# Bias network of a deformable attention: one third-layer matmul for four keys, met by DMA

## The chip, the cores and the metric

The kernel runs on one core of a Trainium2 chip. The metric is the device time of one execution in microseconds (us); lower is better. TensorE (PE), VectorE (DVE), ScalarE (ACT), GpSimd (POOL) and SyncE (SP) each work through their own list of instructions in order. SP and POOL here mostly issue DMAs.

## The reference

Four network layers follow one another on x of shape (2, 512, 32, 32): a deformable attention with an MLP, a linear attention, a non-local block and a squeeze-and-excite block. Only the first one's position bias matters here. For each of 8 groups (4 head pairs x 2 images; the kernel calls one g) there are 64 keys, 512 in all, and 1024 queries, and two heads' queries per key are handled together. For every pair of query and key a small network maps the relative position to a bias:

```python
pos = grid_q[:, :, None, :] - grid_kv[:, None, :, :]
bias = jnp.sign(pos) * jnp.log1p(jnp.abs(pos))
bias = jax.nn.relu(bias @ cpb_w1 + cpb_b1)     # 2 -> 128
bias = jax.nn.relu(bias @ cpb_w2 + cpb_b2)     # 128 -> 128
bias = (bias @ cpb_w3 + cpb_b3)                # 128 -> 1
sim = jnp.einsum('bhid,bhjd->bhij', qh, kh) + bias
attn = jax.nn.softmax(sim, axis=-1)
```

So the third layer is a sum of 128 hidden outputs with weights, for 512 keys x 2048 columns. All is float32.

## The kernel before, in words

**The bias stage.** The loop goes over 256 pairs of keys, `p`. For each key `n`, `first` (L351, VectorE) makes the first layer's 128 x 2048 tile `h1`; `tabp` tables for eight keys at a time are loaded by SP and scaled by ScalarE (L172). For a pair, `second(p, o)` runs four times, for four quarters `o` of the 128 hidden units: two keys x four matmuls into a `ph` tile (L617; 32 output columns of TensorE each, four side by side), then the relu by ScalarE (L626) into a tile `r{o}` of 128 x 2 x 512. The rows of such a tile are 4 column blocks x 32 hidden units, its middle index is the key of the pair. There are 4 buffers for `r0`, 3 for `r2`, one each for `r1` and `r3`.

**Sums before the third layer.** The weights of the third layer have been folded into the second layer and hidden units have been permuted so that units with equal sign of weight stand together. So outputs can simply be added before the last matmul: `combine` (L632, VectorE) adds `r1` to `r0` and `r3` to `r2` with a sign `rel`; `join` (L635) adds `r2` to `r0` by an accumulating DMA on POOL; `shift` (L642, two DMAs on SP) copies half of the rows of each key into a tile `xs` of 128 x 512, and `fold` (L647, two accumulating DMAs on POOL) adds the other half. After that one `xs` tile holds a pair's two keys, interleaved by rows, 16 rows per column block and key. `third(g, u)` (L656) multiplies four `xs` tiles by `cw3`, a narrow matrix of signs, one matmul per pair, four of them into the four 32-row blocks of a `psim` tile.

**The order of work.** Everything in the stage is pinned to program order. The loop runs `second(p, o)` for o = 0 to 3; `first` for the keys of the next pair comes at o = 0 and 2, `combine(p-1, 2)` and `join(p-1)` at o = 1, `combine(p, 0)` at o = 3. All else is put into this loop by a table written by hand: `at(n, when, fn, ...)` places a step at key n (when 0 is after the even o, when 1 after the odd one). Steps placed so are `shift(p)` at key 2p+4, `fold(p)` at 2p+5, `third`, the table loads, the sampling of keys and values for the next group (`prepare`), the softmax of the last group (`attend`: transposes, maxima, exponentials, sums) and the offset network of later groups (`chain`, whose 36 taps at L229 are spread over 80 and 116 keys). `psb` (L584) spreads signs and biases over the 128 rows once at the start; `spread_out` (L480) copies them and makes `cw3`.

After the stage the attention's output projection (L1035), the MLP (L1100) and the other layers follow; they don't touch the change.

Of the kernel before, what the change touches and what calls it, by code (L numbers as in the profile page):

```python
# [27 lines left out]
MID = C // 4  # L28
SE = C // 16
EPS = 1e-5  # L30
FMAX = float(np.finfo(np.float32).max)


# [21 lines left out]

_CONSTS = [("ident", P), ("grid", 2 * J), ("gridf", J), ("npx", 1), ("npy", 8), ("sel3", 2)]

_ORDER = [("same", P), ("below", P), ("place", P), ("rank", 1), ("third", 35)]
_CAT, _n = {}, 0
for _name, _w in _CONSTS:  # L60
    _CAT[_name] = (_n, _w)
# [10 lines left out]
def conv_seq(  # L72
# [61 lines left out]
    with ExitStack() as ctx_l0:  # L134
# [3 lines left out]
        kblk = l0.tile([P, 2, 2, J], F32, name="kblk")  # L138
        vblk = l0.tile([P, 2, 2, J], F32, name="vblk")

        co = l0.tile([P, 2, 2, KC * B * J], F32, name="co")
# [44 lines left out]
        def pin(ins):  # L186
            return tc.keep_in_program_order(ins) if started else ins
# [12 lines left out]
        class Chain:  # L200


            def __init__(self, k0, k1, alloc):
                self.k0, self.n, self.alloc = k0, (k1 - k0) * P, alloc
                self.g = slice(k0 * B, k1 * B)
                self.cs = slice(k0 * P, k1 * P)
                self.sums = {}

            def tile(self, name):
# [123 lines left out]

        w2a = l0.tile([P, 4, 32], F32, name="w2a")
        sb3 = l0.tile([P, 4, 2], F32, name="sb3")
        cw3 = l0.tile([P, 35], F32, name="cw3")
        rel = l0.tile([P, 2], F32, name="rel")

        h1p = ctx_att.enter_context(tc.tile_pool(name="h1p", bufs=4))
# [21 lines left out]
        with tc.tile_pool(name="a", bufs=1) as a, tc.tile_pool(name="aps", bufs=3, space=PSUM) as aps, tc.tile_pool(  # L363
# [80 lines left out]
            def oc(name):  # L444
                at, w = _CAT[name]
                return ordc[:, at : at + w]
# [6 lines left out]
            wide = a.tile([P, 4, 4, 32], F32, name="wide")  # L453
# [6 lines left out]
            def counted():  # L460
                pin(ve.tensor_copy(od[:, 7:9], pcnt))
                pin(ve.tensor_scalar(cpbw, cpbw, maj, None, ALU.mult))


                pin(ve.tensor_scalar(maj, total, 4.0, None, ALU.is_ge))
                pin(ve.tensor_scalar(t0, maj, -1.0, 1.0, ALU.mult, ALU.add))
                pin(ve.tensor_scalar(t1, total, -1.0, 8.0, ALU.mult, ALU.add))
# [109 lines left out]
            for k in range(2, KC):  # L577
                for t in range(NT // 512):
                    flip_x(k, t, (dve, act)[t % 2])
                    if (k, t) == (2, 1):  # L580
                        psb = apk.tile([P, 4, 2], F32, name="psb", tag="pfb4")
# [13 lines left out]
        with tc.tile_pool(name="hid", bufs=3) as hid, tc.tile_pool(name="sm", bufs=1) as sm, tc.tile_pool(name="hps", bufs=2, space=PSUM) as hps, tc.tile_pool(  # L595
# [6 lines left out]
            def at(n, when, fn, *args):  # L602

                todo.setdefault((n, when), []).append((fn, args))
# [44 lines left out]
            def third(g, u):  # L649
                kb, i = divmod(u, 4)  # L650
                p = (g * J + 8 * u) // 2
                if i == 0:
                    psims[g, kb] = sps.tile([P, 512], F32, name=f"psim{kb}")
                for m in range(4):
                    pin(
                        nc.tensor.matmul(  # L656
                            psims[g, kb][m * 32 : (m + 1) * 32, :],
                            lhsT=cw3[:, 3 - i : 35 - i],
                            rhs=rs.pop(p + m),
                            start=(i == 0),  # L660
                            stop=(i == 3),
                            skip_group_check=True,
                        )
                    )

            def prepare(g):

                k, b = divmod(g, B)
                st = {}
                n = J * (g - 1) + 30  # L670
                def hat(t):
                    if t == 0:
                        st["smp"] = smpp.tile([P, 8, 2, J], F32, name="smp")
                    pin(
                        nc.scalar.activation(
                            st["smp"][:, t],
                            co[:, 1, :, g * J : (g + 1) * J],
                            AF.Abs,
                            bias=c("npy")[:, t : t + 1],
                        )  # L680
                    )
# [4 lines left out]

                def cross(i):
                    sp = st["smp"][:, 4 * i : 4 * i + 4]
                    hx = co[:, 0, :, g * J : (g + 1) * J]
# [30 lines left out]
                def keys():  # L720

                    for h in range(2):
                        hs = slice(h * DH, (h + 1) * DH)
                        pin(
                            nc.scalar.activation(
                                kblk[hs, g % 2, h, :].rearrange("p (k x i) -> p k x i", k=2, i=4),
                                st["pk"][hs, 0, :].rearrange("p (k i x) -> p k x i", k=2, i=4),
                                AF.Identity,
                                scale=DH**-0.5,
                            )  # L730
                        )

                def values():
                    for h in range(2):
                        hs = slice(h * DH, (h + 1) * DH)
                        pin(
                            nc.vector.tensor_copy(
                                vblk[hs, g % 2, h, :].rearrange("p (k x i) -> p k x i", k=2, i=4),
                                st["pk"][hs, 1, :].rearrange("p (k i x) -> p k x i", k=2, i=4),
                            )  # L740
                        )

# [154 lines left out]
                    )  # L897
            for g in range(NG):
                prepare(g)
                for u in range(8):  # L900
                    at(J * g + 8 * u + 14, 0, third, g, u)
                if g < NG - 1:
                    attend(g, J * (g + 1) + 7, True)
            for p in range(NK // 2):
                at(2 * p + 4, 0, shift, p)
                at(2 * p + 5, 0, fold, p)

            def chain(k0, k1, n, taken):
                ch = Chain(k0, k1, lambda shape, name: mps.tile(shape, F32, name=name, tag="m"))
# [970 lines left out]
def _layout(a):  # L1880
# [50 lines left out]
    rank = p // 32 * 2 + p % 2  # L1931
    same = p[:, None] % 32 // 2 == p[None] % 32 // 2
    put("same", same.astype(f), order)
    put("below", (same & (rank[:, None] < rank[None])).astype(f), order)
    put("place", np.array([0, 1, 4, 5, 2, 3, 6, 7])[rank].astype(f)[None], order)
    put("rank", rank.astype(f)[:, None], order)
    put("third", (np.arange(35)[None] == (3 + 8 * (p // 32) + 4 * (p % 2))[:, None]).astype(f), order)
    put("npy", -(4 * np.arange(8)[None] + p[:, None] // 32).astype(f))


# [54 lines left out]
```

## Time and profile before

| | us |
|---|---|
| three runs | 2724.93, 2726.71, 2727.19 |
| median | 2726.71 |
| profiled execution, own time | 2726.49 |
| its span, first to last instruction | 2724.7 |
| second-layer matmuls L617, busy | 1781.7 |
| first layer L351, busy | 1171.1 |
| relu L626, busy | 1141.6 |
| combine L632, busy | 656.2 |
| third-layer matmuls L656, busy (512 records) | 70.5 |
| join L635, 256 issues, issue to landing (median) | 4.8 |
| shift L642, 512 issues, issue to landing (median) | 2.2 |
| fold L647, 512 issues, issue to landing (median) | 4.7 |
| TensorE / VectorE / ScalarE / POOL busy, share of span | 98% / 83% / 56% / 25% |

A matmul in float32 leaves two records, so 512 records at L656 are 256 matmuls. Busy time of a group counts the time in which at least one of its instructions ran; records of one engine may overlap, so a sum of records can be more than the time that the engine needs. In lines of groups, the columns are: line, engine, operation, output<-input, shape and count, then busy us, mean ns of one, and idle time before them with what ended it. In timelines a line begins with the start in us and the length in us. The bias stage runs from 44 to about 1942 us at a full TensorE clock.

### The profile page before, as it was taken

How to read it: one execution, taken by the hardware profiler on the slowest of the kernel's cores; microseconds unless marked ns; L12 is line 12 of the kernel's file. 1: busy time of each engine (PE TensorE's matmuls, PEld its weight loads, DVE VectorE, ACT ScalarE, POOL GpSimd, SP SyncE). 2: the span in 40 equal slices, each digit the busy share in tenths (PEclk: the TensorE clock that was granted, in tenths of full speed). 3: DMA queues.
4: the chain of work that ended last, by engine and by line, in shares of the span. 5: the costliest groups of instructions: out<-in, count | busy, mean ns of one | idle time of the engine just before them, and what ended most of it. 6: DMA issues, size and time to landing. Idle time of an engine off the chain costs nothing.

```text
span 2724.7 us, 49360 instructions
## 1 busy us (share of the span) xinstructions
PE 2681.3 (98%) x19830; PEld 978.1 (36%) x19830; DVE 2253.8 (83%) x1993; ACT 1538.4 (56%) x1904; POOL 670.2 (25%) x784
## 2 busy tenths in 40 slices
PE   8999999999999999999999999999999999999997
PEld 4223323232332323333333233333344444455544
DVE  6999999999999999999999999999554544615646
ACT  7676687667668766866766776776221111001334
POOL 0333333333333333333333333333100000000001
PEclk9999999999999999999999999999999999999998
DMA  3777777877777787777787788787410000100001
GB/s 128 165 167 164 161 157 156 172 154 161 168 155 160 155 174 155 161 167 157 168 193 164 157 174 189 156 172 157 94 30 23 16 23 24 39 38 1 0 0 62
DMA packets 146196, 335.13 MB, mean 123 GB/s; under 512 B 22672, under 2 KB 32400, under 8 KB 145200
## 3 DMA queue, kind: packets, MB, share of 16 engines
q0 software_dynamic: 77824, 201.38, 41.5%
q1 hardware_dynamic: 67568, 130.08, 13.6%
q8 instruction: 157, 2.57, 0.4%
q14 instruction: 71, 0.58, 0.1%
q10 hardware_dynamic: 576, 0.51, 0.1%
HBM read 58.99 MB, written 4.46 MB: 23 GB/s over the span
## 4 chain that ended last, share of the span: by engine, by line
PE 89%; DVE 6%; issue 3%; ACT 2%; DMA 0%; DVEq 0%; POOL 0%; ACTq 0%; POOLq 0%
PE ph L617 58%; PE A L1100 4%; PE D L1100 4%; PE C L1100 4%; PE B L1100 2%; PE psim L656 2%; PE po L1035 2%; DVE h L351 2%; DVE r L632 2%; PE pg L1243 1%; PE pa L1354 1%; PE pu L1277 1%; PE pscore L1486 1%; PE pz L1515 1%; PE pt L1506 1%
## 5 line engine op out<-in xcount | busy, mean ns | idle before, releaser
L617 PE MATMUL ph<-h,w2a 128*32 128x512 f32 x16384 | 1781.7, 592 | 4.3 <-ACT r L626 3.6
L626 ACT ACTIVATE r<-ph,sb 128x1024 f32<-128x1024 f32 x1024 | 1141.6, 1115 | 533.2 <-PE ph L617 508.1
L351 DVE CUSTOM_DVE_ANT_1 h<-tab 128x2048 f32<-128x2048 f32 x512 | 1171.1, 2287 | 22.4 <-PE ph L617 17.7
L617 PEld LDWEIGHTS ph<-h,w2a 128*32 128x32 f32 x16384 | 522.2, 109 | 1219.8 <-issue 832.0
L632 DVE SCALAR_TENSOR_TENSOR r<-r,rel,r 128x1024 f32<-128x1024 f32 x512 | 656.2, 1282 | 26.8 <-ACT r L626 26.5
L647 POOL DMA_DIRECT2D xs<-r x512 | 475.0, 1128 | 225.7 <-DMA xs<-r 122.7
L635 POOL DMA_DIRECT2D r<-r x256 | 222.6, 869 | 1047.8 <-DVE r L632 874.5
L172 ACT ACTIVATE tab<-tab,vec 128x256 f32<-128x256 f32 x252 | 137.1, 544 | 0.0
L1288 POOL MEMSET M<- 128x512 f32 x2 | 1.0, 518 | 443.8 <-DVE x L1164 443.8
L1140 ACT COPY u<-A 128x512 f32<-128x512 f32 x16 | 9.4, 586 | 146.9 <-PE A L1100 146.9
L1771 POOL TENSOR_TENSOR x<-x,aff 128x512 f32<-128x512 f32 x7 | 7.0, 1029 | 329.1 <-ACT e L1736 329.1
L1119 ACT ACTIVATE h<-h,vec 128x512 f32<-128x512 f32 x32 | 23.1, 721 | 113.6 <-DVE h L1122 113.6
L656 PE MATMUL psim<-xs,cw 128*32 128x512 f32 x512 | 70.5, 594 | 2.2 <-DMA xs<-r 2.2
L1122 DVE TENSOR_TENSOR h<-C,u 128x512 f32<-128x512 f32 x32 | 22.1, 691 | 47.7 <-PE C L1100 47.4
L1100 PE MATMUL A<-xn,w 128*128 128x512 f32 x128 | 60.3, 593 | 0.8 <-DVE x L1042 0.8
L1100 PE MATMUL C<-hT,w 128*128 128x512 f32 x128 | 60.3, 592 | 0.0
L1100 PE MATMUL A<-h,w 128*128 128x512 f32 x128 | 60.1, 592 | 0.0
L1035 PE MATMUL po<-q,vwo 128*128 128x512 f32 x128 | 57.1, 599 | 0.0
L229 DVE SCALAR_TENSOR_TENSOR acc<-q,vec,acc 128x128 f32<-128x128 f32 (+3 forms) x88 | 45.9, 521 | 0.8
L1160 DVE TENSOR_TENSOR x<-D,x 128x512 f32<-128x512 f32 x32 | 22.1, 691 | 26.0 <-PE D L1100 26.0
L852 ACT ACTIVATE e<-e,den 128x64 f32<-128x64 f32 x128 | 41.8, 337 | 2.2 <-DVE den L848 2.2
L1160 DVE TENSOR_TENSOR x<-C,x 128x512 f32<-128x512 f32 x32 | 22.1, 691 | 24.8 <-PE C L1100 24.8
(364 smaller groups left out, 1840.3 us busy)
## 6 DMA issues: line engine op xcount, KB each, us to landing
r<-r POOLq DMA_DIRECT2D x256, 512.0 KB, 4.8
xs<-r SPq DMA_DIRECT2D x512, 128.0 KB, 2.2
xs<-r POOLq DMA_DIRECT2D x512, 128.0 KB, 4.7
tab<-fd SPq DMA_DIRECT2D x63, 512.0 KB, 6.2
lw<-in_l_w_dram SPq DMA_DIRECT2D x5, 1024.0 KB, 9.1
x<-in_x_dram SPq DMA_DIRECT2D x4, 1024.0 KB, 9.0
w<-in_mlp_w_dram SPq DMA_DIRECT2D x8, 512.0 KB, 4.4
w<-in_mlp_w_dram SPq DMA_DIRECT2D x16, 256.0 KB, 3.2
```

The costliest lines, as they stand in the source:

```text
L172: return nc.scalar.activation(tf, tf if src is None else src[:, :, ax, :], AF.Identity, bias=0.0 if ax == 0 else v("L0_conv_cpb_b1"), scal ...
L229: pin(nc.vector.scalar_tensor_tensor(dst, src, wt_, dst, ALU.mult, ALU.add))
L351: nc.vector._custom_dve(TENSOR_ADD_SAT, out=h1, in0=columns.unsqueeze(1).to_broadcast([P, 32, 2, 32]), in1=rows_.unsqueeze(3).to_broadcast ...
L617: nc.tensor.matmul(ph[t * 32 : (t + 1) * 32, i, :], lhsT=w2a[:, o], rhs=h1s[2 * p + i][:, half * 16 : (half + 1) * 16, h, :], start=True, ...
L626: pin(nc.scalar.activation(r, ph, AF.Relu, bias=sb3[:, o, 1:2]))
L632: pin(nc.vector.scalar_tensor_tensor(r0, r1, rel[:, i : i + 1], r0, ALU.mult, ALU.add))
L635: pin(nc.gpsimd.dma_start(rs[p, 0], rs.pop((p, 2)), accum_op=ALU.add))
L647: pin(nc.gpsimd.dma_start(rs[p][i::2], r[i::2, i, :], accum_op=ALU.add))
L656: nc.tensor.matmul(psims[g, kb][m * 32 : (m + 1) * 32, :], lhsT=cw3[:, 3 - i : 35 - i], rhs=rs.pop(p + m), start=(i == 0), stop=(i == 3), ...
L1035: nc.tensor.matmul(po, lhsT=vwo[:, k * B + t // 2, o * P : (o + 1) * P], rhs=q[:, k, ts_], start=(k == 0), stop=(k == KC - 1),)
L1100: nc.tensor.matmul(banks[bank], lhsT=a[an][k], rhs=b_[bn_][k], start=(i < 4 and k == 0), stop=(k == n - 1), skip_group_check=True,)
L1160: nc.vector.tensor_tensor(to, t, to, ALU.add)
```

## The change

Neighbouring hidden units are summed once more before the third layer. `shift` and `fold` now take other rows: the odd rows of a key are copied and the even rows added, and key i of the pair goes into the 64 adjacent rows 64i to 64i+63 of `xs`. A new step `meet` then joins two neighbouring pairs, a (even p) and b (odd p), in three DMAs: step 0 adds a's odd rows to a's even rows (POOL), step 1 copies b's even rows into a's odd rows (SP), step 2 adds b's odd rows there (POOL). After it one `xs` tile holds four keys, eight rows per column block and key, and `third` runs one matmul on it: it is called every 16 keys instead of 8. The last four pairs don't meet; they go into the third layer alone, with a second matrix `cw3d`. For that the hidden units are sorted in classes of 16 instead of 8. The tile `xs` becomes two: `xs0` with 6 buffers and `xs1` with 2 instead of 5 of one kind; a coordinate table `co` is cut from four to three parts to make room. The softmax, the sampling and the second chain's steps are placed five keys later; the first chain's taps are spread over 85 keys.

```diff
-                xs = rs[p] = hid.tile([P, 512], F32, name="xs", bufs=5)
+                xs = rs[p] = hid.tile([P, 512], F32, name=f"xs{p % 2}", bufs=(6, 2)[p % 2])
                 for i in range(2):
-                    pin(nc.sync.dma_start(xs[i::2], r[1 - i :: 2, i, :]))
+                    pin(nc.sync.dma_start(xs[64 * i : 64 * i + 64], r[1::2, i, :]))
 
             def fold(p):
                 r = rs.pop((p, 0))
                 for i in range(2):
-                    pin(nc.gpsimd.dma_start(rs[p][i::2], r[i::2, i, :], accum_op=ALU.add))
+                    pin(nc.gpsimd.dma_start(rs[p][64 * i : 64 * i + 64], r[0::2, i, :], accum_op=ALU.add))
+
+            def meet(p, step):
+
+                a, b = rs[p], rs[p + 1]
+                if step == 0:
+                    pin(nc.gpsimd.dma_start(a[0::2], a[1::2], accum_op=ALU.add))
+                elif step == 1:
+                    pin(nc.sync.dma_start(a[1::2], b[0::2]))
+                else:
+                    pin(nc.gpsimd.dma_start(a[1::2], b[1::2], accum_op=ALU.add))
+                    rs.pop(p + 1)
 
             def third(g, u):
-                kb, i = divmod(u, 4)
-                p = (g * J + 8 * u) // 2
+                kb, i = divmod(u, 2)
+                p = (g * J + 16 * u) // 2
...
+                for m in range(4):
+                    alone = p + 2 * m >= NK // 2 - 4
+                    w = cw3d[:, 5 - i : 37 - i] if alone else cw3[:, 1 - i : 33 - i]
+                    add(m, w, p + 2 * m, i == 1 and not alone)
+                for m in range(4):
+                    if p + 2 * m + 1 in rs:
+                        add(m, cw3d[:, 1 - i : 33 - i], p + 2 * m + 1, True)
...
-                n = J * (g - 1) + 30
+                n = J * (g - 1) + 35
...
-                for u in range(8):
-                    at(J * g + 8 * u + 14, 0, third, g, u)
+                for u in range(4):
+                    at(J * g + 16 * u + 27, 0, third, g, u)
                 if g < NG - 1:
-                    attend(g, J * (g + 1) + 7, True)
+                    attend(g, J * (g + 1) + 12, True)
             for p in range(NK // 2):
                 at(2 * p + 4, 0, shift, p)
                 at(2 * p + 5, 0, fold, p)
+
+                if p % 2 and p < NK // 2 - 4:
+                    at(2 * p + 6, 1, meet, p - 1, 0)
+                    at(2 * p + 8, 0, meet, p - 1, 1)
+                    at(2 * p + 9, 1, meet, p - 1, 2)
...
-            chain(1, 2, 84, 80)
-            chain(2, 4, 211, 116)
+            chain(1, 2, 89, 85)
+            chain(2, 4, 216, 116)
```

At the start, `psb` gets a fifth matmul and with it a fifth copy in `wide`, and `spread_out` one more scaling:

```diff
-                pin(ve.tensor_copy(wide, to))
+                pin(ve.tensor_copy(wide[:, 0:4], to))
...
+                pin(
+                    ve.tensor_copy(
+                        wide[:, 4].rearrange("p t o -> p (t o)").rearrange("p (a b c) -> p a b c", a=8, b=8), to
+                    )
+                )
...
-                pin(ve.tensor_scalar(cw3, oc("third"), sb3[:, 0, 0:1], None, ALU.mult))
+                pin(ve.tensor_scalar(cw3, oc("third"), sb3[:, 4, 0:1], None, ALU.mult))
+                pin(ve.tensor_scalar(cw3d, oc("direct"), sb3[:, 4, 0:1], None, ALU.mult))
...
-                        for o in range(4):
+                        for o in range(5):
```

What is left out here is the constants made on the host (`same`, `place`, `third`, `direct`: which class a hidden unit belongs to, which column of the matrix a row adds to), the sorting by signs with 8 and 16 in the place of 4 and 8, the addresses in `co`, and the order of keys inside `kblk` and `vblk`.

More of the change, by code (lines that the diff above doesn't have):

```diff
@@ L30 @@
 EPS = 1e-5
+CO_AT = (1, 0, 1, 2)
 FMAX = float(np.finfo(np.float32).max)
@@ L56 @@
 _CONSTS = [("ident", P), ("grid", 2 * J), ("gridf", J), ("npx", 1), ("npy", 8), ("sel3", 2)]
-_ORDER = [("same", P), ("below", P), ("place", P), ("rank", 1), ("third", 35)]
+_ORDER = [("same", P), ("below", P), ("place", P), ("rank", 1), ("third", 33), ("direct", 37)]
 _CAT, _n = {}, 0
@@ L139, in conv_seq @@
         vblk = l0.tile([P, 2, 2, J], F32, name="vblk")
-        co = l0.tile([P, 2, 2, KC * B * J], F32, name="co")
+        co = l0.tile([P, 2, 2, 3 * B * J], F32, name="co")
         kvw = l0.tile([P, 2, KC, P], F32, name="kvw")
@@ L205, in __init__ @@
                 self.g = slice(k0 * B, k1 * B)
-                self.cs = slice(k0 * P, k1 * P)
+                self.cs = slice(CO_AT[k0] * P, (CO_AT[k0] + k1 - k0) * P)
                 self.sums = {}
@@ L336, in conv_seq @@
         w2a = l0.tile([P, 4, 32], F32, name="w2a")
-        sb3 = l0.tile([P, 4, 2], F32, name="sb3")
-        cw3 = l0.tile([P, 35], F32, name="cw3")
+        sb3 = l0.tile([P, 5, 2], F32, name="sb3")
+        cw3 = l0.tile([P, 33], F32, name="cw3")
+        cw3d = l0.tile([P, 37], F32, name="cw3d")
         rel = l0.tile([P, 2], F32, name="rel")
@@ L452, in conv_seq @@
             perm = a.tile([P, P], F32, name="perm")
-            wide = a.tile([P, 4, 4, 32], F32, name="wide")
+            wide = a.tile([P, 5, 4, 32], F32, name="wide")
             ve = nc.vector
@@ L462, in counted @@
                 pin(ve.tensor_scalar(cpbw, cpbw, maj, None, ALU.mult))
-                pin(ve.tensor_scalar(maj, total, 4.0, None, ALU.is_ge))
+                pin(ve.tensor_scalar(maj, total, 8.0, None, ALU.is_ge))
                 pin(ve.tensor_scalar(t0, maj, -1.0, 1.0, ALU.mult, ALU.add))
-                pin(ve.tensor_scalar(t1, total, -1.0, 8.0, ALU.mult, ALU.add))
+                pin(ve.tensor_scalar(t1, total, -1.0, 16.0, ALU.mult, ALU.add))
                 pin(ve.scalar_tensor_tensor(t0, t1, t0, below, ALU.mult, ALU.add))
@@ L477, in placed @@
                 to = perm.rearrange("p (s o) -> p s o", s=4).unsqueeze(2).to_broadcast([P, 4, 4, 32])
-                pin(ve.tensor_copy(wide, to))
+                pin(ve.tensor_copy(wide[:, 0:4], to))
+                to = perm[:, 0:32:4].unsqueeze(1).unsqueeze(3).to_broadcast([P, 8, 8, 2])
+                pin(
[3 more added lines that the diff above has]
+                )
             def spread_out():
@@ L580, in conv_seq @@
                     if (k, t) == (2, 1):
-                        psb = apk.tile([P, 4, 2], F32, name="psb", tag="pfb4")
-                        for o in range(4):
+                        psb = apk.tile([P, 5, 2], F32, name="psb", tag="pfb4")
+                        for o in range(5):
                             to = wide[:, o].rearrange("p t o -> p (t o)")
@@ L646, in fold, with add @@
                 for i in range(2):
-                    pin(nc.gpsimd.dma_start(rs[p][i::2], r[i::2, i, :], accum_op=ALU.add))
+                    pin(nc.gpsimd.dma_start(rs[p][64 * i : 64 * i + 64], r[0::2, i, :], accum_op=ALU.add))
[8 more added lines that the diff above has]
+                    rs.pop(p + 1)
             def third(g, u):
-                kb, i = divmod(u, 4)
-                p = (g * J + 8 * u) // 2
+                kb, i = divmod(u, 2)
+                p = (g * J + 16 * u) // 2
                 if i == 0:
                     psims[g, kb] = sps.tile([P, 512], F32, name=f"psim{kb}")
-                for m in range(4):
+                def add(m, w, p, stop):
                     pin(
@@ L657, in third @@
                             psims[g, kb][m * 32 : (m + 1) * 32, :],
-                            lhsT=cw3[:, 3 - i : 35 - i],
-                            rhs=rs.pop(p + m),
+                            lhsT=w,
+                            rhs=rs.pop(p),
                             start=(i == 0),
-                            stop=(i == 3),
+                            stop=stop,
                             skip_group_check=True,
@@ L669, in prepare @@
                 st = {}
-                n = J * (g - 1) + 30
+                n = J * (g - 1) + 35
+                here = slice(CO_AT[k] * P + b * J, CO_AT[k] * P + (b + 1) * J)
                 def hat(t):
@@ L676, in hat @@
                             st["smp"][:, t],
-                            co[:, 1, :, g * J : (g + 1) * J],
+                            co[:, 1, :, here],
                             AF.Abs,
@@ L688, in cross @@
                     sp = st["smp"][:, 4 * i : 4 * i + 4]
-                    hx = co[:, 0, :, g * J : (g + 1) * J]
+                    hx = co[:, 0, :, here]
                     pin(nc.vector.tensor_tensor(sp, sp, hx.unsqueeze(1).to_broadcast([P, 4, 2, J]), ALU.mult))
@@ L725, in keys @@
                             nc.scalar.activation(
-                                kblk[hs, g % 2, h, :].rearrange("p (k x i) -> p k x i", k=2, i=4),
-                                st["pk"][hs, 0, :].rearrange("p (k i x) -> p k x i", k=2, i=4),
+                                kblk[hs, g % 2, h, :].rearrange("p (k x i) -> p k x i", k=2, i=2),
+                                st["pk"][hs, 0, :].rearrange("p (k i x) -> p k x i", k=2, i=2),
                                 AF.Identity,
@@ L737, in values @@
                             nc.vector.tensor_copy(
-                                vblk[hs, g % 2, h, :].rearrange("p (k x i) -> p k x i", k=2, i=4),
-                                st["pk"][hs, 1, :].rearrange("p (k i x) -> p k x i", k=2, i=4),
+                                vblk[hs, g % 2, h, :].rearrange("p (k x i) -> p k x i", k=2, i=2),
+                                st["pk"][hs, 1, :].rearrange("p (k i x) -> p k x i", k=2, i=2),
                             )
@@ L1929, in _layout @@
     put("sel3", (p[:, None] % 32 == np.array([1, 2])[None]).astype(f))
-    rank = p // 32 * 2 + p % 2
-    same = p[:, None] % 32 // 2 == p[None] % 32 // 2
+    rank = p // 32 * 4 + p % 4
+    same = p[:, None] % 32 // 4 == p[None] % 32 // 4
     put("same", same.astype(f), order)
     put("below", (same & (rank[:, None] < rank[None])).astype(f), order)
-    put("place", np.array([0, 1, 4, 5, 2, 3, 6, 7])[rank].astype(f)[None], order)
+    put("place", (np.array([0, 2, 1, 3])[p // 32] * 4 + p % 4).astype(f)[None], order)
     put("rank", rank.astype(f)[:, None], order)
-    put("third", (np.arange(35)[None] == (3 + 8 * (p // 32) + 4 * (p % 2))[:, None]).astype(f), order)
+    column = 1 + 8 * (p % 64 // 16) + 2 * (p % 2 * 2 + p // 64)
+    put("third", (np.arange(33)[None] == column[:, None]).astype(f), order)
+    column = 5 + 8 * (p % 64 // 16) + 2 * (p // 64)
+    put("direct", (np.arange(37)[None] == column[:, None]).astype(f), order)
     put("npy", -(4 * np.arange(8)[None] + p[:, None] // 32).astype(f))
```

## The prediction

> **What bounds the kernel now.** The chain of waits comes first: 58% of the span is the second-layer matmul at L617 and 2% the third-layer matmul at L656. All of that lies in the bias stage, about 44 to 1942 us. Next, the table of stretches (busy us of each engine, the granted clock, the mean DMA share, GB/s):
>
> ```profile
> 60.00:300.00 240.00, 239.84 (x2236) 72.35 (x2228) 238.87 (x172) 167.96 (x183) 85.16 (x99) 1.00 0.76 164
> 300.00:600.00 300.00, 298.11 (x2761) 93.73 (x2757) 294.38 (x209) 216.18 (x256) 103.21 (x120) 1.00 0.75 159
> 600.00:900.00 300.00, 298.31 (x2750) 91.90 (x2743) 295.08 (x204) 219.89 (x276) 104.03 (x121) 1.00 0.75 162
> 900.00:1200.00 300.00, 299.46 (x2808) 93.27 (x2804) 287.29 (x181) 213.15 (x246) 105.36 (x123) 1.00 0.76 161
> 1200.00:1500.00 300.00, 300.00 (x2800) 94.61 (x2794) 287.40 (x178) 212.70 (x244) 105.28 (x124) 1.00 0.78 170
> 1500.00:1800.00 300.00, 300.00 (x2802) 92.92 (x2798) 291.12 (x184) 216.51 (x256) 107.49 (x126) 1.00 0.79 170
> 1800.00:1900.00 100.00, 100.00 (x936) 30.54 (x932) 96.55 (x57) 71.47 (x82) 36.07 (x43) 1.00 0.77 164
> ```
>
> TensorE (first) is full, but VectorE (third) is nearly so: idle 240 - 238.87 = 1.1 us in the first stretch, 5.6 + 4.9 = 10.5 in the next two, 12.7 + 12.6 + 8.9 + 3.4 = 37.6 after 900. TensorE's time can only fall by what VectorE can follow. ScalarE (fourth) is 72% busy. Then the timelines of TensorE and VectorE:
>
> ```profile
> 508.96 1.04 PE L656 MATMUL psim<-xs,cw 128*32 128x512 f32 x8
> 509.82 27.65 PE L617 MATMUL ph<-h,w2a 128*32 128x512 f32 x256
> 537.28 1.04 PE L656 MATMUL psim<-xs,cw 128*32 128x512 f32 x8
> ```
>
> ```profile
> 131.61 2.29 DVE L351 CUSTOM_DVE_ANT_1 h<-tab 128x2048 f32<-128x2048 f32 x1
> 133.81 1.28 DVE L632 SCALAR_TENSOR_TENSOR r<-r,rel,r 128x1024 f32<-128x1024 f32 x1
> 135.01 0.43 DVE L229 SCALAR_TENSOR_TENSOR acc<-q,vec,acc 128x128 f32<-128x128 f32 x1
> ```
>
> Start to start, a third-layer group of four matmuls (eight records) occupies TensorE for 509.82 - 508.96 = 0.86 us, and eight keys of layer two for 27.46: 28.32 us per eight keys. VectorE needs 2.20 for L351 and 1.20 for L632 per key: 27.2 per eight keys.
>
> [...] L656's records sum to 70.5 us over 64 groups (1.10 each), but the next start comes after 0.86, the price I use. [...]
>
> **The change, part by part.**
>
> *Third layer.* Its instruction list has 130 matmuls where there were 256: 32 groups of four plus two. Removed: 126/4 = 31.5 groups x 0.86 = 27.1 us of TensorE. By the counts of L656 in the stretches, half of 8 groups falls before 300 (3.4 us), half of 20 before 900 (8.6), half of 34 after (14.6); the rest is in the tail, where the last folds set the end.
>
> What VectorE allows: while the offset taps (L229) run, eight keys hold 3.6 taps at 0.35 (first chain) or 2.5 at about 0.58 (second). That is 27.2 + 1.3 or 1.4 = 28.5 to 28.6 us, already above TensorE's 28.3 and far above the new 27.46 + 0.43 = 27.9. Up to about 800 us VectorE therefore keeps the pace. I take 0.3 of 3.4 before 300 and 4 of 8.6 up to 900, because part of the 10.5 us of idle is a wait for one block of TensorE transposes per 64 keys and stays. After 900 there are no taps, and VectorE has 37.6 us idle against 14.6 wanted. Per 64 keys the softmax bunches four passes of about 0.6 us into five keys and TensorE has less filler for it to catch up behind; I take off 0.4 for each of the four spans of 64 keys: 13.0. Sum: 17.3 us.
>
> *Moved work.* Softmax, sampling and second-chain steps come five keys later, the first chain's taps spread over 85 keys instead of 80. Same instructions, same engines, still inside the loop: 0. Shorter vectors cw3, other permutations: 0.
>
> *Start.* One more copy (L476, same size: 0.29), one more scaling (L483: 0.24, 0.08 of it start to start), one more psb matmul (0.95/4 = 0.24). All lie in the chain there: +0.5.
>
> *New DMAs.* Three for 126 pairs of pairs: 252 accumulating ones of 0.131 MB on POOL (33.0 MB), 126 copies on SP (16.5 MB). The queue table prices them:
>
> ```profile
> q0 software_dynamic: 77824, 201.38, 41.5%
> q1 hardware_dynamic: 67568, 130.08, 13.6%
> ```
>
> q0: 0.415 x 2724.7 / 201.38 = 5.6 us of all 16 engines per MB, so 185 us. q1: 2.85 per MB, 47 us. The stretches hold 1408 us of DMA in 1840 (77%); 1408 + 232 = 1640 in some 1823 is 90%. POOL issues 252 more at up to 1.13 us (L647): 647 + 285 = 932 of 1823. Room on both, if packets keep their length.
>
> *Waits added.* On SP, meet's copy waits for the landing of meet's first accumulate, issued right behind a join. It should land 0.7 us (185/252) after the join; behind it wait the next shift (every second one) and then on POOL its fold, the second accumulate and the following join. With the copy's own issue (0.5) and packets (0.4) that fold is about 1.7 us late. It frees the r0 buffer (4 of them) that ScalarE's L626 writes four pairs later. Over the pairs of this trace a pair's second fold is issued 10.7 us before that write (8.3 at the shortest twentieth) and lands in about 4.7: 6.0 us of slack, 3.6 at the twentieth. So it fits, but a fuller DMA queue eats the rest. Lower bound 0, since nothing here shortens a wait on TensorE's path; upper bound in C. I take +1.5. Meet's second accumulate is issued about 10 us before its third-layer matmul: 0.
>
> Sum: -17.3 + 0.5 + 1.5 = -15.3. The profiled execution took 2726.49 (span 2724.7), 0.2 under the median 2726.71, so the median moves to **2711**; this case's own range is 2703 to 2719.
>
> **Rivals.**
> A. All 27.1 arrives: VectorE's idle is spare and catches up everywhere. For it: TensorE shows no wait for VectorE above 11 us in total (L632 10.8). Against it: 1.1 us of idle before 300. 2726.7 - 27.1 + 0.5 = 2700. Chance 0.12.
> B. The saving is used up by late folds or by VectorE's lag: 2722 to 2732. Chance 0.12.
> C. Slower: DMA becomes the bound. The change also turns the target of shift and fold from every second partition into 64 adjacent ones. q1 now moves 130.08 MB / 371 us = 351 GB/s; [...] It decides once landings slip by more than the 4 us of slack, at roughly 100% DMA share. Against it: today's 351 GB/s is reached by DMAs that also have only 64 rows, and two of them, for the two halves, follow each other at once. Chance 0.22.
> That the change does not cut the matmuls is excluded by its instruction list. The likeliest case has 0.54.
>
> **How the numbers follow.** A measurement of this kernel can tell about 0.2% (5.5 us) from no change. Faster: A and the likeliest case, 0.66. Same: B, 0.12. Slower: C, 0.22. The range leaves out the far half of C and a little of A: 2698 to 2740.
>
> **What would show it.** L656 with 260 records and about 36 us; DMA share near 0.90; VectorE's idle before 900 below 8 us, TensorE below 100% there, with waits of L617 for VectorE or for L626; after 900 eight keys at 27.9 us on average. Wrong if shift landings go from 2.2 to over 3.5 us, folds and joins past 7, and L626 waits for a DMA (C), or if VectorE's idle stays near 49 us while TensorE waits.

## The result, and the profile after

The changed kernel takes **2898.4 us** (median of 4 runs, 2889.64 to 2901.98) against 2726.5 for the kernel before on the same chip (4 runs, 2724.93 to 2727.19): ratio 1.0627, 95% interval 1.0602 to 1.0651. It is 172 us slower, where 2711 was forecast. The profiled execution took 2889.64, with a span of 2887.8.

The lines have moved: join is L646, shift L653, fold L658, the meets' steps L664 (POOL), L666 (SP) and L668 (POOL), relu L637, combine L643, first layer L354, second layer L628, third layer L679. The chain of waits of the changed kernel, by engine and by line:

```profile
DMA 42%; PE 36%; issue 7%; DVE 6%; POOL 5%; ACT 3%; SPq 1%; POOLq 0%; DVEq 0%; ACTq 0%
DMA xs<-r 22%; DMA xs<-xs 20%; PE ph L628 10%; PE A L1138 4%; PE D L1138 4%; PE C L1138 4%; POOL xs L658 4%; DVE h L354 3%; PE po L1073 2%; PE B L1138 2%; ACT r L637 1%; PE pg L1281 1%; DVE r L643 1%; SPq L666 1%; PE pa L1392 1%
```

Before, the second layer carried 58% of the span. Now it carries 10%, and 42% are transfers, half of them the meets (xs<-xs). The table of stretches (busy us of TensorE, weight load, VectorE, ScalarE, POOL, then clock, DMA share, GB/s):

```profile
300.00:900.00 600.00, 560.67 (x5051) 169.48 (x5044) 555.03 (x384) 394.44 (x465) 264.91 (x303) 0.98 0.87 174
900.00:1800.00 900.00, 835.78 (x7566) 252.95 (x7562) 794.19 (x499) 591.92 (x715) 391.83 (x448) 0.98 0.88 178
```

TensorE and VectorE both stand idle now (39 and 45 us of the first stretch's 600), and TensorE does not wait for VectorE. The waits, with what ended them (us in total, times, longest); the last line is of the kernel before:

```profile
POOL xs L658 <- DMA xs<-r: 1063.7, 131, 12.4
ACT r L637 <- DMA xs<-r: 190.0, 70, 7.0
PE ph L628 <- ACT r L637: 138.1, 82, 5.3
...
POOL xs L647 <- DMA xs<-r: 122.7, 82, 6.9
```

Read from TensorE's wait upwards: TensorE waits for the relu, the relu for the fold that frees its r0 buffer, and the fold's issue on POOL for the landing of the shift. Queues and landings (packets, MB, share; then count, KB, us to landing):

```profile
q0 software_dynamic: 97984, 234.42, 48.6%
q1 hardware_dynamic: 77648, 146.62, 15.3%
...
r<-r POOLq DMA_DIRECT2D x256, 512.0 KB, 7.9
xs<-r SPq DMA_DIRECT2D x512, 128.0 KB, 3.4
xs<-r POOLq DMA_DIRECT2D x512, 128.0 KB, 6.5
xs<-xs POOLq DMA_DIRECT2D x252, 128.0 KB, 6.5
xs<-xs SPq DMA_DIRECT2D x126, 128.0 KB, 5.0
```

Join, shift and fold landed in 4.8, 2.2 and 4.7 us before. POOL's timeline shows what repeats (start, length; in brackets the idle time ahead and what ended it):

```profile
1017.78 0.83 POOL L658 DMA_DIRECT2D xs<-r  x1 [8.28 <-DMA xs<-r]
1018.83 0.84 POOL L658 DMA_DIRECT2D xs<-r  x1 [0.22 <-issue]
1019.38 1.17 POOL L668 DMA_DIRECT2D xs<-xs  x1
1019.91 1.55 POOL L646 DMA_DIRECT2D r<-r  x1
1020.48 1.85 POOL L664 DMA_DIRECT2D xs<-xs  x1
1021.00 3.06 POOL L658 DMA_DIRECT2D xs<-r  x2
1023.78 1.19 POOL L646 DMA_DIRECT2D r<-r  x1
1033.52 0.83 POOL L658 DMA_DIRECT2D xs<-r  x1 [8.54 <-DMA xs<-r]
...
1037.03 1.85 POOL L664 DMA_DIRECT2D xs<-xs  x1
```

and SP's, at the same time:

```profile
1027.94 0.47 SPq L666 DMA_DIRECT2D xs<-xs  x1
1028.57 5.09 SPq L653 DMA_DIRECT2D xs<-r  x4
```

This is a ring. Step 0 is issued at 1020.48 and lands at 1027.93; the copy that waited for it goes out on SP, and only then the next shift (1028.57), for which POOL's fold waits; behind that fold stand step 2, the join and the next step 0, at 1037.03: 16.55 us for four keys. At the pace of the forecast, without TensorE's other work, they need 27.9/2 = 13.9. Over the whole stage the 126 first steps (L664) go out from 80.0 to 2072.4 us, one every 15.9 us. Eight POOL issues (four folds, two meets, two joins) fall into one burst of 7 us, and the DMA engines follow it (TensorE busy, clock, DMA share, GB/s, in stretches of 4 us):

```profile
1019.00:1023.00 4.00, 4.00 (x44) 1.00 1.01 217
1023.00:1027.00 4.00, 4.00 (x40) 1.00 1.07 186
1027.00:1031.00 4.00, 4.00 (x44) 1.00 1.06 207
1031.00:1035.00 4.00, 4.00 (x40) 1.00 0.47 144
```

Twelve us full (a share slightly above 1 is read as full), then four at half: the mean of 0.87 hides that the engines are full and then starved.

### The profile page after: what moved, and what is told of

Same layout as the page of the kernel before. It is cut to its first block, busy times and chain, and to the rows that moved or that the text cites. A ratio compares the mean times of both kernels' runs of the same rounds, so it can differ in the third digit from the quotient of the medians.

```text
span 2887.8 us, 49675 instructions
## 1 busy us (share of the span) xinstructions
PE 2703.7 (94%) x19580; PEld 967.0 (33%) x19580; DVE 2263.8 (78%) x1995; ACT 1526.8 (53%) x1904; POOL 902.1 (31%) x1036
## 4 chain that ended last, share of the span: by engine, by line
DMA 42%; PE 36%; issue 7%; DVE 6%; POOL 5%; ACT 3%; SPq 1%; POOLq 0%; DVEq 0%; ACTq 0%
DMA xs<-r 22%; DMA xs<-xs 20%; PE ph L628 10%; PE A L1138 4%; PE D L1138 4%; PE C L1138 4%; POOL xs L658 4%; DVE h L354 3%; PE po L1073 2%; PE B L1138 2%; ACT r L637 1%; PE pg L1281 1%; DVE r L643 1%; SPq L666 1%; PE pa L1392 1%
## 5 line engine op out<-in xcount | busy, mean ns | idle before, releaser
L628 PE MATMUL ph<-h,w2a 128*32 128x512 f32 x16384 | 1824.0, 602 | 138.5 <-ACT r L637 138.1
L637 ACT ACTIVATE r<-ph,sb 128x1024 f32<-128x1024 f32 x1024 | 1135.8, 1113 | 700.4 <-PE ph L628 484.8
L354 DVE CUSTOM_DVE_ANT_1 h<-tab 128x2048 f32<-128x2048 f32 x512 | 1170.1, 2286 | 85.7 <-PE ph L628 84.0
L628 PEld LDWEIGHTS ph<-h,w2a 128*32 128x32 f32 x16384 | 519.3, 111 | 1405.3 <-issue 831.5
L658 POOL DMA_DIRECT2D xs<-r x512 | 629.0, 1737 | 1077.8 <-DMA xs<-r 1063.7
L643 DVE SCALAR_TENSOR_TENSOR r<-r,rel,r 128x1024 f32<-128x1024 f32 x512 | 655.1, 1280 | 111.2 <-ACT r L637 110.2
L646 POOL DMA_DIRECT2D r<-r x256 | 437.4, 1709 | 126.1 <-DVE r L643 114.7
L664 POOL DMA_DIRECT2D xs<-xs x126 | 263.1, 2088 | 0.0
L668 POOL DMA_DIRECT2D xs<-xs x126 | 183.2, 1454 | 0.7 <-issue 0.7
L679 PE MATMUL psim<-xs,cw 128*32 128x512 f32 x252 | 35.1, 596 | 9.4 <-DMA xs<-xs 9.4
```

The costliest lines, as they stand in the source:

```text
L354: nc.vector._custom_dve(TENSOR_ADD_SAT, out=h1, in0=columns.unsqueeze(1).to_broadcast([P, 32, 2, 32]), in1=rows_.unsqueeze(3).to_broadcast ...
L628: nc.tensor.matmul(ph[t * 32 : (t + 1) * 32, i, :], lhsT=w2a[:, o], rhs=h1s[2 * p + i][:, half * 16 : (half + 1) * 16, h, :], start=True, ...
L637: pin(nc.scalar.activation(r, ph, AF.Relu, bias=sb3[:, o, 1:2]))
L643: pin(nc.vector.scalar_tensor_tensor(r0, r1, rel[:, i : i + 1], r0, ALU.mult, ALU.add))
L646: pin(nc.gpsimd.dma_start(rs[p, 0], rs.pop((p, 2)), accum_op=ALU.add))
L658: pin(nc.gpsimd.dma_start(rs[p][64 * i : 64 * i + 64], r[0::2, i, :], accum_op=ALU.add))
```

## Experiments

Medians in us; ratios to the kernel before on the same chip, estimated from all runs, so that they can differ slightly from the quotient of the medians. The quoted expectations number their theories anew for each round.

### First round: waits, traffic or rows

**no_meet**: `meet` issues nothing and only drops b's tile.

```diff
-                    pin(nc.gpsimd.dma_start(a[0::2], a[1::2], accum_op=ALU.add))
...
-                    pin(nc.sync.dma_start(a[1::2], b[0::2]))
...
-                    pin(nc.gpsimd.dma_start(a[1::2], b[1::2], accum_op=ALU.add))
```

> The changed kernel without the three DMAs of meet; it leaves out the meeting, so the odd pairs' sums never reach the third layer. All else (130 third-layer matmuls, the new rows of shift and fold, the shifted schedule) stays. Theory 1 (the in-order waits around meet set the pace) and theory 2 (the extra DMA traffic fills the engines): both expect the forecast's gain to appear, 2700 to 2720 us. Theory 3 (the 64 adjacent rows slow shift and fold): stays at or above 2800. It also measures the step of the forecast that VectorE lets only about 17 of 27 us through: 2709 if so, 2699 if all arrives.

2704.2 (2702.1 to 2706.9), ratio 0.9920 (0.9906 to 0.9935). The loss needs the meets.

**half_rows**: the kernel before, with the new rows of shift and fold alone.

```diff
-                    pin(nc.sync.dma_start(xs[i::2], r[1 - i :: 2, i, :]))
+                    pin(nc.sync.dma_start(xs[64 * i : 64 * i + 64], r[1::2, i, :]))
...
-                    pin(nc.gpsimd.dma_start(rs[p][i::2], r[i::2, i, :], accum_op=ALU.add))
+                    pin(nc.gpsimd.dma_start(rs[p][64 * i : 64 * i + 64], r[0::2, i, :], accum_op=ALU.add))
```

> The kernel before with only the new rows in shift and fold (targets are 64 adjacent partitions, sources odd and even rows); its third layer then weighs other hidden units than it should. Theories 1 and 2: within 0.5% of the kernel before (2714 to 2740), shift packets as before, landing 2.2 and 4.7 us. Theory 3 [...]: shift landing above 3 us, over 2% slower.

2728.4 (2726.9 to 2730.3), ratio 1.0010 (1.0002 to 1.0019): alone, the rows cost hardly anything. But its queue table shows what they do:

```profile
q0 software_dynamic: 77824, 201.38, 46.4%
q1 hardware_dynamic: 67568, 130.08, 13.7%
```

The same bytes as before take 0.464 x 2727.2 = 1265 us of the 16 engines on q0 instead of 1131, and 374 instead of 371 on q1. So with 64 adjacent rows the accumulating transfers take longer (+134 us) and the plain copies hardly, though a shift now lands in 3.0 us instead of 2.2. It costs 3 us here. The new folds also read other rows than those they write, where before they read the same ones. That alone is not it: in no_meet_full_rows (third round) half of the folds do so too, in every second row, and q0 takes 0.418 x 2697.2 = 1127 us. No run separates adjacent rows from rows far from their source.

**meet_aside**: the meets' transfers, equal in size, queue and place, between tiles that nobody else waits for.

```diff
-                a, b = rs[p], rs[p + 1]
+                a = vwo[:, 6 + p // 2 % 2, :] if p < NK // 4 else wo[:, p // 2 % 2, :]
+                b = kvw.rearrange("p i k c -> p (i k c)")[:, 0:512]
...
-                    pin(nc.gpsimd.dma_start(a[0::2], a[1::2], accum_op=ALU.add))
+                    pin(nc.gpsimd.dma_start(a[0::2], b[1::2], accum_op=ALU.add))
...
-                    pin(nc.gpsimd.dma_start(a[1::2], b[1::2], accum_op=ALU.add))
+                    pin(nc.gpsimd.dma_start(a[0::2], b[1::2], accum_op=ALU.add))
```

> The changed kernel with meet's three DMAs of the same sizes, from the same queues at the same places in the program, but between tiles that nobody waits for (dead slices of the projection weights), so the met sums are left out. Theory 1 (a ring of waits: first accumulate, copy on SP, next shift, next fold, next first accumulate): 2705 to 2740 us, DMA share near 0.90, POOL's wait for shifts back to some 150 us. Theory 2 (the engines are full): 2850 or more with landings of 6 us and over. Theory 3: as the changed kernel, about 2890.

2869.8 (2844.9 to 2885.4), ratio 1.0519 (1.0458 to 1.0580). Without the data waits only 29 us come back: POOL still waits for the shifts,

```profile
POOL xs L659 <- DMA xs<-r: 953.2, 169, 13.7
```

and the shifts for the joins (SP 1418.3 us in all; in the changed kernel 246.9, where the copy waited ahead of them). So the ring also closes without the copy, over join, shift, fold and the next join. I read the loss that stays as the price of the traffic, which the last run showed to be wrong.

**copy_later**: one wait moved. The copy goes on SP behind the next shift.

```diff
-                    at(2 * p + 8, 0, meet, p - 1, 1)
+                    at(2 * p + 8, 1, meet, p - 1, 1)
```

> The changed kernel with one number altered: meet's copy on SP stands half a key later, behind the next shift instead of ahead of it. Same DMAs, same bytes. Theory 1: the ring is cut, the shift no longer waits for the first accumulate; well below the changed kernel, 2710 to 2800 us (the second accumulate may now make POOL wait). Theories 2 and 3: within 1% of 2898.

2824.6 (2800.2 to 2838.2), ratio 1.0343 (1.0280 to 1.0405): 74 us back for a transposition of two instructions on SP. The ring is real, but cutting it there leaves 98.

### Second round: every second row again

**full_rows** and **aside_full_rows**: the changed kernel and meet_aside with the rows of before.

```diff
-                    pin(nc.sync.dma_start(xs[64 * i : 64 * i + 64], r[1::2, i, :]))
+                    pin(nc.sync.dma_start(xs[i::2], r[1::2, i, :]))
...
-                    pin(nc.gpsimd.dma_start(rs[p][64 * i : 64 * i + 64], r[0::2, i, :], accum_op=ALU.add))
+                    pin(nc.gpsimd.dma_start(rs[p][i::2], r[0::2, i, :], accum_op=ALU.add))
```

> The changed kernel whole, but shift and fold write every second row of xs (xs[i::2]) as the kernel before does, instead of 64 adjacent rows. The meets then add rows of two different keys, which leaves their time the same; only the time is read. Theory 1 (the new rows lengthen the folds' packets and the meets' traffic comes on top; together they fill the DMA engines): the 2048-byte accumulating packets fall from 687 us of the 16 engines to about 550, fold landings from 6.5 to about 5 us, and the time from 2898 to 2720 to 2790. Theory 2 (the meets' traffic alone is too much, whatever the rows): 2850 to 2900. Theory 3 (the ring of in-order queues, copy ahead of the next shift, sets a period of its own): 2820 to 2870, with POOL still waiting some 8 us at a fold every four keys.

2785.3 (2783.2 to 2790.6), ratio 1.0222 (1.0207 to 1.0238).

> As meet_aside (the meets' transfers run between tiles that nobody waits for), with every second row of xs in shift and fold. Left out of the computation: the meets. Theory 1: packets short again, 2700 to 2740, so that the rows were worth 130 us or more under this traffic. Theory 2: 2830 to 2870, as meet_aside's 2870. Theory 3 says that with no data waits the traffic costs little once the packets are short, and puts the difference between this run and full_rows at over 60 us; theory 1 puts it at under 50.

2714.5 (2710.4 to 2722.0), ratio 0.9963 (0.9949 to 0.9977). With every second row the data waits cost 71 us, and the same traffic without them 10 over no_meet (15 over no_meet_full_rows below, which has the same rows). The rows, worth 3 us alone, are worth 113 and 155 under the meets.

**full_32** and **full_32_later**: the same rows, with each step as two transfers of 32 rows, so that the sums meet the right keys. In these two the third layer's weights still stood in the row order of 64-row meets; only their times are read.

```diff
-                    pin(nc.gpsimd.dma_start(a[0::2], a[1::2], accum_op=ALU.add))
+                    for i in range(2):
+                        pin(nc.gpsimd.dma_start(a[i::4], a[i + 2 :: 4], accum_op=ALU.add))
...
+                        pin(nc.sync.dma_start(a[i + 2 :: 4], b[i::4]))
...
+                        pin(nc.gpsimd.dma_start(a[i + 2 :: 4], b[i + 2 :: 4], accum_op=ALU.add))
```

> The whole change with every second row of xs in shift and fold, and each meet step in two transfers of 32 rows, every fourth row (a[i::4] += a[i+2::4], a[i+2::4] <- b[i::4], a[i+2::4] += b[i+2::4]), the third layer's column constants set to that order: computes the reference. Twice as many meet transfers, each of half the bytes. Theory 1: within 30 us of full_rows, so 2700 to 2800. Theory 2: 2850 to 2920. Theory 3: the two issues for one lengthen the ring by 1 to 2 us per four keys, 60 to 120 us over full_rows.

2831.4 (2824.4 to 2838.1), ratio 1.0397 (1.0379 to 1.0414): 46 over full_rows, with twice as many meet issues of half the size.

> As full_32, with the meets' copy issued on SP behind the next shift (2p+8, 1) instead of ahead of it. Theory 1: 2690 to 2740; with short packets the order matters by under 40 us. Theory 2: 2790 to 2840, as copy_later's 2825. Theory 3: 70 us or more below full_32.

2740.9 (2736.3 to 2743.2), ratio 1.0054 (1.0039 to 1.0069): 90 us for the order of the copy.

### Third round: places

**full_32_spread** and **after_spread**: other places for the steps, in the 32-row version (from here on with the weights in its own row order) and in the changed kernel.

```diff
-                    at(2 * p + 6, 1, meet, p - 1, 0)
-                    at(2 * p + 8, 0, meet, p - 1, 1)
-                    at(2 * p + 9, 1, meet, p - 1, 2)
+                    at(2 * p + 8, 1, meet, p - 1, 0)
+                    at(2 * p + 8, 1, meet, p - 1, 1)
+                    at(2 * p + 10, 1, meet, p - 1, 2)
```

> The whole change with every second row of xs, 32-row meet transfers (the third layer's weights per row now in that order too), and the meets' issues moved by the trace of full_32_later: there POOL waits 5 to 7 us at every second fold and then issues two folds, two meets, two joins and two meets in a burst. Step 0 goes into that wait (2p+8, 1: ahead of the fold that waits), the copy behind it on SP, step 2 behind the join of the burst (2p+10, 1). Theory 1 (short packets, and the order of the two queues decides the rest): 2705 to 2725, POOL's wait at the folds below 420 us (full_32_later: 473). Theory 2 (the DMA engines' traffic sets what is left over aside_full_rows' 2714): 2735 to 2745, as full_32_later. A step 2 that waits for the copy would show as POOL waiting at the second meet, and give 2740 to 2780.

2769.1 (2766.8 to 2784.8), ratio 1.0176 (1.0152 to 1.0200): a miss, 28 slower than full_32_later. SP's queue in its waits says why:

```profile
SPq L653 <- DMA xs<-xs: 685.3, 126, 8.8
```

Every fourth key a shift waits for a meet. The tile b has two buffers (`xs1`), and step 2, now later, keeps it until the shift of the next but one odd pair wants it. A later place had lengthened a buffer's life.

> The changed kernel with only the meets' places changed as in full_32_spread (64 adjacent rows stay). If order alone were the cause: below 2740. By theory 1 the lengthened fold packets and the traffic stay: between copy_later's 2825 and 60 us less, and slower than before in any case.

2887.9 (2885.2 to 2894.7), ratio 1.0590 (1.0574 to 1.0607): no help either, and a miss, as the expected gain did not come.

**no_meet_full_rows**: no_meet with every second row.

> The changed kernel without the meets' transfers (the sum of the other rows is left out) and with every second row of xs: what the third layer's saving is worth when neither rows nor meets cost anything. Theory 1: 2690 to 2704 (no_meet with adjacent rows 2704), so that with short packets the meets' traffic costs 10 to 25 us (aside_full_rows 2714). If the rows are harmless without the meets, within 4 us of no_meet.

2699.2 (2697.7 to 2699.5), ratio 0.9900 (0.9887 to 0.9914): this is what the third layer's saving is worth by itself, 27.1 us.

### Fourth round: the steps early

**early_steps** (32 rows, every second row) and **after_early** (the changed kernel) move the steps ahead: step 0 needs only a's fold, and the copy's data are there before the next shift's.

```diff
-                    at(2 * p + 6, 1, meet, p - 1, 0)
-                    at(2 * p + 8, 0, meet, p - 1, 1)
-                    at(2 * p + 9, 1, meet, p - 1, 2)
+                    at(2 * p + 4, 1, meet, p - 1, 0)
+                    at(2 * p + 7, 1, meet, p - 1, 1)
+                    at(2 * p + 8, 1, meet, p - 1, 2)
```

> As full_32_spread (whole change, every second row, 32-row meet transfers), with other places: step 0, which needs only the first pair's fold, ahead of the second pair's fold on POOL (2p+4, 1); the copy on SP ahead of the next shift again, but now its data are there before that shift's (2p+7, 1); step 2 on POOL ahead of the fold two pairs on (2p+8, 1). All meet issues so lie in POOL's 6 us wait before every second fold, and the second buffer is free sooner than in any run so far. Theory 1 (order and buffers): 2705 to 2730, SP's shifts waiting for meets below 60 us. Theory 2 (the dependent transfers cost by themselves, in landings of 5 us each whatever the order): 2735 to 2770.

**2701.1** (2700.5 to 2701.4), ratio 0.9910 (0.9895 to 0.9925): a little below the range expected: 24 us faster than the kernel before, and 2 to 3 slower than no_meet_full_rows (2 by the medians, 3 by each one's kernel before). It makes all the sums of the changed kernel, and beats both kernels. POOL's timeline:

```profile
1004.94 0.86 POOL L646 DMA_DIRECT2D r<-r  x1 [3.00 <-DVE r L643]
1005.48 2.02 POOL L671 DMA_DIRECT2D xs<-xs  x2
1006.54 2.66 POOL L665 DMA_DIRECT2D xs<-xs  x2
1008.65 2.31 POOL L658 DMA_DIRECT2D xs<-r  x2
1011.81 0.86 POOL L646 DMA_DIRECT2D r<-r  x1 [0.85 <-DVE r L643]
1013.90 1.75 POOL L658 DMA_DIRECT2D xs<-r  x2 [1.23 <-DMA xs<-r]
1018.68 0.86 POOL L646 DMA_DIRECT2D r<-r  x1 [3.03 <-DVE r L643]
```

The meets (L671, L665) stand right behind a join, in the time in which POOL had waited for the shift; a join now waits for its own input (VectorE), not for the queue, and the ring shown takes 1018.68 - 1004.94 = 13.7 us. Over the stage it is one every 14.5 us (first steps, L665, from 72.6 to 1884.5). POOL's wait for the shifts, the stretches and the landings:

```profile
POOL xs L658 <- DMA xs<-r: 110.2, 74, 5.7
```

```profile
300.00:900.00 600.00, 594.94 (x5487) 184.12 (x5483) 596.39 (x418) 438.45 (x531) 351.01 (x410) 1.00 0.90 190
900.00:1800.00 900.00, 899.32 (x8400) 280.47 (x8396) 874.60 (x547) 651.00 (x759) 532.83 (x623) 1.00 0.92 196
```

```profile
r<-r POOLq DMA_DIRECT2D x256, 512.0 KB, 4.9
xs<-r SPq DMA_DIRECT2D x512, 128.0 KB, 3.2
xs<-r POOLq DMA_DIRECT2D x512, 128.0 KB, 5.0
```

The DMA share is higher than in the changed kernel (0.90 and 0.92 against 0.87 and 0.88), and joins and folds land nearly as fast as before.

> The changed kernel with 64 adjacent rows and 64-row meets, only the meets' places changed as in early_steps. Theory 1: the traffic on lengthened packets stays, which by meet_aside was 166 us over no_meet: 2800 to 2870. Under 2760 would say that order was the cause and adjacent rows hardly mattered.

2746.3 (2741.4 to 2750.1), ratio 1.0081 (1.0064 to 1.0098): a miss for theory 1. The places alone, with adjacent rows and all data waits, take back 152 of the 172 us.

**aside_early**: meet_aside with these places.

> meet_aside (64 adjacent rows; the meets' transfers of equal size between tiles that nobody waits for; the meets themselves left out) with the places of after_early (2p+4,1; 2p+7,1; 2p+8,1). If the places decide: 2725 to 2750, as after_early's 2746 or a little below, with the DMA share at 0.90 or more. If the traffic decides: 2840 to 2880, as meet_aside's 2870.

2731.1 (2722.6 to 2752.4), ratio 1.0027 (1.0013 to 1.0041). The same transfers that took 2870 at the old places cost 139 us less here, and joins land in 5.9 us instead of 7.8. So most of what meet_aside measured was the place of these transfers, not their bytes: 27 us over no_meet are left.

## Why the prediction was wrong, by its own steps

Taken back one after the other, the difference splits over four runs: from before's 2726.3 the third layer takes 27.1 (no_meet_full_rows, 2699.2); the meets in their best places add 2 (early_steps, 2701.1); the adjacent rows, with 64-row meets, add 45 (after_early, 2746.3); the places at which the change put the steps add 152 (2898.4). The shares depend on the order: with every second row the places are worth 130 (full_32 against early_steps), and at the old places the rows are worth 113 (full_rows).

**Waits added, +1.5: the step that failed.** It measured about 152 with the adjacent rows and 130 without them. It saw a ring of waits, and 6.0 us of slack, but priced one wait alone: a copy 0.7 us behind the join's landing. In the ring shown the step that the copy waits for lands 7.45 us after its issue. What it left out is that the change adds two issues to POOL exactly behind the wait for the shift, so that four folds, two meets and two joins leave in 7 us on one queue. The join then lands after 7.9 us instead of 4.8, the shift waits for it and for the copy, and the next burst comes later still. At equal bytes joins take 7.8 us in meet_aside, where a meet is issued just ahead of every second one, and 5.9 in aside_early, where the meets stand behind the joins. The runs show that the place decides; by what means inside the queue was not shown. The slack of 6 us had been read from a trace in which the landings were short. In the changed kernel join, shift and fold land 3.1, 1.2 and 1.8 us later than before, 6.1 together, as much as the whole slack.

**New DMAs: "room on both, if packets keep their length".** The forecast of 232 us holds: early_steps spends 0.492 x 2699.2 = 1328 us on q0 and 421 on q1, against 1131 and 371 before, so +197 and +50 (forecast 185 and 47). The condition does not hold with adjacent rows: in half_rows q0, which carries the folds, takes 134 us more for the same bytes, and q1, which carries the shifts, 3. Rival C had looked at these rows; what they would cost was the author's estimate and not shown by the trace before.

**Rival C** had the sign. Its full engines fit after_early: DMA share 0.96 in the stretches, 21 us slower than before. Of the signs that it named, the relu's wait for a DMA came (190.0 us) and the joins' landing (7.9); shifts (3.4) and folds (6.5) stopped just short. It decides "at roughly 100% DMA share", though, and the changed kernel lost its 172 us at 0.87. A mean share under 1 proves no room where the transfers come in bursts: this is what "room on both" overlooked.

**Third layer, 17.3 of 27.1: too low.** L679 has the 260 records that were forecast, 252 of them 35.1 us, and in no_meet_full_rows the gain is all of the 27.1 us; rival A's size was right. Its stretches read (VectorE is the third busy time)

```profile
300.00:900.00 600.00, 594.92 (x5487) 184.09 (x5482) 596.23 (x419) 438.43 (x531) 211.38 (x246) 1.00 0.76 163
900.00:1800.00 900.00, 899.47 (x8400) 280.61 (x8396) 874.91 (x547) 651.83 (x760) 320.80 (x375) 1.00 0.78 169
```

so its idle time from 300 to 900 fell from 10.5 to 3.8 us, where I had kept more than half of it for waits that would stay, and after 900 nothing had to be taken off for bunched softmax passes.

**Start, +0.5, and moved work, 0**: not measured apart. The start's three parts, 0.29, 0.08 and 0.24, make 0.6 and not 0.5. Both must be small, as the 27.1 leave nothing over.

Why the parts don't add up: rows alone cost 3 us (half_rows), traffic alone 15 (aside_full_rows over no_meet_full_rows), both at the old places 171 (meet_aside over no_meet_full_rows). I read this as the ring's slack: little is paid until it is longer than TensorE's time for its four keys (14.5 us on average in early_steps), and the rest of it afterwards. In the changed kernel it takes 15.9: about 1.45 us more for each of 126 rings, some 180 of the 197 us between the two. Why the new rows lengthen accumulating transfers and not plain copies stays open.

## What to carry to other kernels

Before you add a DMA to an in-order queue, write down what is issued in the few microseconds around it and which of those somebody waits for; put it in a wait that the queue has anyway, behind the urgent transfers (early_steps, 130 us faster than full_32), and check whose buffer then lives longer (full_32_spread, where the shifts waited 685.3 us for meets). Read the DMA share in stretches shorter than the loop's period: a mean of 0.87 was a ring of full and half-empty engines, and 0.92 ran faster. Slack read from a trace is slack at that trace's landings: 6.0 us of it here, and 6.1 us of later landings.

## What the runs showed of the hardware that I had not expected

Some waits of TensorE cost more than their length. After one for a relu the granted clock falls (timeline; then busy, clock, DMA share, GB/s):

```profile
311.52 7.48 PE L628 MATMUL ph<-h,w2a 128*32 128x512 f32 x68
321.25 9.18 PE L628 MATMUL ph<-h,w2a 128*32 128x512 f32 x68 [2.25 <-ACT r L637]
...
316.00:320.00 4.00, 3.00 (x28) 1.00 1.06 246
320.00:324.00 4.00, 2.75 (x16) 0.66 1.05 176
324.00:328.00 4.00, 4.00 (x40) 0.91 0.99 207
328.00:332.00 4.00, 4.00 (x44) 1.00 0.46 125
```

The clock records of this trace show 20 such falls between 60 and 1900 us, each to half the clock for 3.41 us (twice for 6.8), and all 20 begin whole multiples of 3.41 us apart. Cut the time into pieces of that length, at the beginnings of the falls: each of the 17 pieces in which TensorE idled for 2.0 us or more was followed by a fall, no fall began after one with less than 1.69, and of those between some were followed by one. So a single wait of 3.2 us that lay in two pieces cost no clock, and one of 1.73 us within one piece did. The second layer's matmuls are busy for 1824.0 us in all instead of 1781.7, so 42 of the 172 us show up as slower matmuls and not as idle time; 22 x 3.41 us at half the clock make 38 of them. The second layer's matmuls take up to 1064 ns in a fall; their median is 592.
